# A gated cross-attention and feed-forward layer: the last attention step divided straight into the last two token tiles, and a new list for the end

## The chip, the cores and the metric

The kernel runs on one core of a Trainium2 chip, as one program. The metric is device time in microseconds (us). A core has a matrix engine (PE; its weight loads are shown as PEld), a vector engine (DVE), a scalar engine for activations (ACT), a general engine (POOL) and a queue that issues transfers (SP). Each takes its own instructions strictly in order, and they wait for each other through semaphores. PE writes to PSUM; everything else lies in SBUF or in the chip's main memory.

## The reference

Two gated residual steps over `x` of 32 sequences, 224 tokens, 512 channels, with a context of 750 keys of 384 channels:

```python
x = x + tanh(g_xattn[0]) * xattn(layernorm(x), ctx, mask, Wq, Wkv)   # 16 heads of 32
x = x + tanh(g_ffn[0])   * ffn(layernorm(x), w1, b1, w2, b2)         # 512 -> 2048 -> 512

def bitlinear(x, w, b):
    xq = act_quant(rmsnorm(x))      # 8 bit steps, one scale for each token
    wq = weight_quant(w)            # -1, 0, 1 times one scale
    return einsum('bsd,fd->bsf', xq, wq) + b
def ffn(x, ...): return bitlinear(gelu(bitlinear(x, w1, b1)), w2, b2)
```

Attention of a sequence needs nothing of the others; the feed-forward part works on each token alone.

## The kernel before

**Attention.** A step is one sequence `b` and one group `g` of four heads: 128 steps, numbered 0 to 127. A step has three score rounds. In each, `maxima` computes scores with the queries on the partitions, and DVE takes their row maxima (`mx`); `weights` computes them again with the keys on the partitions, adds the negative maxima (`nT`, turned by `turn_max`), and ACT takes the exponential (`p`), which POOL adds up into `acc`. Both kinds of scores (`sm` and `se` in the profile) use one PSUM tile in turn. `values` multiplies `p` with the values into `po`; `sums` adds `acc` over the partitions with a product with ones, DVE transposes the result to `oT` and takes the reciprocals `rd`; `finish` divides on POOL into `yo`, and `store` writes `yo` with four transfers to the scratch tensor `o_d` in main memory. The main loop (line 1005) interleaves the maxima of step n+1, the weights of step n, the values of step n-1, and the projections of later sequences (`pk`, `pv`, `pq`) in six slots of each step.

**Feed-forward.** The 7168 tokens form 56 tiles of 128, taken in 28 pairs (0 to 27). `ffn_units` gives the work of a pair as named units: `load` of `x` and `o_d` into `xg` and `og`, `add`, `stats`, `rsqrt`, `norm`, `max`, `sa0` to `sa2` (scales), `grid`, `bias`, `round`, `turn` (two transposing transfers), all for both tiles at once; then for each tile t the four column blocks `bt0` to `bt3` of the first product, each evicted by DVE into `h`, `gelut`, `squaret`, `hmt0`, `hmt1` (maxima of the halves), `sbt0` to `sbt2`, `cgridt`, `croundt`, `cturnt`, two halves `ct0` and `ct1` of the second product, and `outt`. The last two pairs borrow tiles of the attention: `x` and `o_d` of pair 27 lie in one tile (`xo` in the profile), and its normalised values and their rounded form in another (`xc`).

**What sets the order.** `Ffn.fill` (line 857) is called in each slot and places units while the slot has room on PE, ACT and DVE. `late` (line 890) widens PE's room by how many tiles are waiting beyond an allowance: 3 everywhere. GELU and exponential need different function tables on ACT, so a `gelu` in the main loop loads one table, computes, and loads the other one back.

After step 126's loop, `drain` (line 895) writes out everything that is left as one list: the weights of step 127 (`top`, `w0` to `w2`), values and sums of steps 126 and 127 (`val`, `vlast`), their divisions and stores (`fin0`, `sto0`, `fin1`, `sto1`), and all units left of pairs 25, 26 and 27. It keeps a clock for each engine, looks up in `TAKES_US` how long each unit takes and on which engine it may run, and takes one unit after the other: among those that can start soonest, the one with the longest chain behind it (`rank`). Where a unit can run on DVE or on POOL or ACT, `small[0]` tells the unit which. `LAST` holds what the units of the attention wait for, `behind` what the units of a pair wait for besides the unit ahead of them. The `fetch` of pair 27's part of `o_d` waits for `sto1`, the last store.

The helper class `Ordered` (line 52 is its call) records every operation, so nearly all instructions in the profile have line 52.

Of the kernel before, what the change touches and what calls it, by code (L numbers as in the profile page):

```python
# [8 lines left out]
F32 = mybir.dt.float32  # L9
# [15 lines left out]
def flamingo_gated_layer(  # L25
# [410 lines left out]
    def finish(b, g):  # L436
# [6 lines left out]
        yo_of[b, g] = yo  # L443

    def store(b, g):
        yo = yo_of.pop((b, g))
        for j in range(HG):
            cols = slice(g * P + j * DH, g * P + (j + 1) * DH)
            sp.dma_start(
                o_d[b * S : (b + 1) * S, cols].rearrange("(c r) d -> r c d", r=DH),  # L450
                yo[j * DH : (j + 1) * DH],
            )
# [67 lines left out]


    draining = []
    NTI = NT // P
    TG = 2
    NF = NTI // TG

    def quant_scales(s, r, amax, n, tag, unit):

        a = smf.tile([P, n], F32, tag=f"{tag}_am", name=f"{tag}_am")
        c = smf.tile([P, n], F32, tag=f"{tag}_c", name=f"{tag}_c")
        s[tag] = c, a
        if n == 1:
            small[0].tensor_scalar(a, amax, r, 1e-5, ALU.mult, ALU.max)
        else:
            small[0].tensor_tensor(a, r, amax, ALU.mult)
            small[0].tensor_scalar(a, a, 1e-5, None, ALU.max)
        yield  # L540
        dve.reciprocal(c, a)
        yield
        if n == 1:
            small[0].tensor_scalar(c, c, 127.0, r, ALU.mult, ALU.mult)
        else:
            small[0].tensor_scalar(c, c, 127.0, None, ALU.mult)
            small[0].tensor_tensor(c, c, r, ALU.mult)
        small[0].tensor_scalar(a, a, unit, None, ALU.mult)
# [7 lines left out]
    def ffn_units(i):  # L556
# [6 lines left out]
        def a_load():  # L563
            if i >= NF - 2:
                both = yp.tile([P, NYC * M], F32, tag="y", name=f"xo_{i}")
                both = both[:, : 2 * TG * D].rearrange("p (a t d) -> p a t d", a=2, t=TG)
                s["xg"], s["og"] = both[:, 0], both[:, 1]
            else:
                s["xg"] = xgp.tile([P, TG, D], F32, tag="xg", name=f"xg_{i}")
                s["og"] = ogp.tile([P, TG, D], F32, tag="og", name=f"og_{i}")  # L570
# [7 lines left out]
        def a_fetch():  # L578
            sp.dma_start(s["og"], o_d[rows, :].rearrange("(t p) d -> p t d", p=P))

# [19 lines left out]
        def a_norm():  # L600
            if i < NF - 2:
                s["xc"] = fp.tile([P, TG, D], F32, tag="xc", name=f"xc_{i}")
            else:
                both = vp.tile([P, NKC * D // 2], F32, tag="v", name=f"xc_{i}")
                s["xc"] = both[:, : TG * D].rearrange("p (t d) -> p t d", t=TG)
                s["xq"] = both[:, TG * D :].bitcast(BF16).rearrange("p (t d) -> p t d", t=TG)
            for t in range(TG):
# [41 lines left out]
        def b_matmul(t, f):  # L649
# [11 lines left out]
            for k in range(NDC):  # L661
# [4 lines left out]
            dve.scalar_tensor_tensor(  # L666
                s["h", t][:, cols], ph, s["qa"][1][:, t : t + 1], b1_sb[:, cols],
                ALU.mult, ALU.add,
# [63 lines left out]
        ]  # L732
        if i == NF - 1:
            first[1:] = [("fetch", 0, "load", 0, 0, 0, a_fetch), ("add", 0, "fetch", 0, 0, 0, a_add)]
        first += [
# [10 lines left out]
            ("turn", 0, "round", 0, 0, 0, a_turn),  # L746
        ]
        parts = [first]
        for t in range(TG):
            part = []  # L750
            for f in range(4):
                part.append((
                    f"b{t}{f}", 0 if f else 3, f"b{t}{f - 1}" if f else "turn", 0.9, 0, 0.75,
                    lambda t=t, f=f: b_matmul(t, f),
# [33 lines left out]
        "sb2": [[("DVE", 0.4)], [("POOL", 0.6)]], "cgrid": [[("DVE", 1.7)], [("POOL", 2.0)]],  # L788
        "cround": [[("ACT", 2.0)], [("DVE", 1.8)]], "cturn": [[("SP", 3.8)]],
        "c": [[("PE", 1.75), ("DVE", 0.5)]], "out": [[("SP", 2.0)]],  # L790
        "top": [[("PE", 0.3), ("ACT", 0.4)]],
        "w": [[("PE", 1.1), ("ACT", 1.7)]],
        "val": [[("PE", 2.9), ("DVE", 0.9)]], "vlast": [[("PE", 4.0), ("DVE", 0.9)]],
        "fin": [[("POOL", 0.6)]], "sto": [[("SP", 3.6)]],
    }

    QUEUE_US = {"sto": 1.9, "turn": 1.9, "cturn": 1.5, "load": 0.5, "fetch": 0.5, "out": 0.4}

# [3 lines left out]
        for name, after in {  # L802
            "w0": "top", "w1": "w0", "w2": "w1", "val": "", "fin0": "val", "sto0": "fin0",
            "vlast": "w2 val", "fin1": "vlast fin0", "sto1": "fin1 sto0",
        }.items()
    }

    class Ffn:
# [3 lines left out]
        def __init__(self):  # L812
            self.slot = 0
            self.parts = []
            self.next = 0
            self.at = {}

        def behind(self, pair, name):
# [3 lines left out]
                "load": [(pair - XG, f"out{TG - 1}"), (pair - 1, "add")],  # L822
                "fetch": [(NF, "sto1")],
                "norm": [(pair - 1, "round")],
# [5 lines left out]
            if name[-1].isdigit():  # L830
                t = int(name[len(name.rstrip("0123456789"))])
                (p1, t1), (ph, th) = (divmod(pair * TG + t - n, TG) for n in (1, HB))
                before = {
                    f"b{t}0": [(pair, "turn")]
                    + [(ph - (pair == NF - 1), f"cround{th}")] * (pair != NF - 2),
# [12 lines left out]
        def ready(self, pair, unit):  # L848
            name, lag, after = unit[:3]
            lag = lag if not draining else 0  # L850
            if after is not None:
# [38 lines left out]
        def late(self, stored, more):  # L890

            ready = stored * S // P - TG * self.next + sum(p[1][-1][0][:3] == "out" for p in self.parts)
            return 0.3 * max(0, ready - (LATE if stored < B - 8 else 3) - more)

        def drain(self, more):
# [3 lines left out]
            draining.append(True)  # L899
            free = {"PE": 0.0, "ACT": 0.0, "DVE": 4.3, "POOL": 5.0, "SP": 0.0}  # L900
            end = {}

            def takes(name):
                kind = name.rstrip("0123456789")
                return TAKES_US.get(kind) or TAKES_US[kind + name[-1]]

            self.parts.insert(0, [NF, more])
            while self.next < NF:
                self.parts += [[self.next, part] for part in ffn_units(self.next)]
                self.next += 1  # L910
            left = {}

            def rank(at):

                if at not in left:
                    left[at] = 0.0
                    left[at] = sum(us for _, us in takes(at[1])[0]) + max(
                        (rank(x) for x in behind if at in behind[x]), default=0.0
                    )
                return left[at]  # L920

            behind = {
                (pair, u[0]): [(pair, u[2] or "")] + self.behind(pair, u[0])
                for pair, units in self.parts for u in units
            }

            def course(at, way):

                t = max(
                    [end.get(x, 0.0) for x in behind[at]  # L930
                     if x[1].rstrip("0123456789") not in ORDER_ONLY or x[1][:-1] != at[1][:-1]],
                    default=0.0,
                )
                t = begin = max(t, free[way[0][0]])
                for engine, us in way:
                    t = max(t, free[engine]) + us
                return begin, t

            while self.parts:
                self.slot += 10  # L940
                found = []
                for part in self.parts:
                    for unit in part[1]:
                        if self.ready(part[0], unit):
                            at = part[0], unit[0]
                            way = min(
                                takes(unit[0]), key=lambda way: course(at, way)[1]
                                + 1.0 * sum(us for engine, us in way if engine == "DVE"),
                            )
                            found.append((course(at, way)[0], -rank(at), part, unit, way))  # L950
                soon = min(f[0] for f in found) + 2
                t, _, part, unit, way = min((f for f in found if f[0] <= soon), key=lambda f: f[1])
                part[1].remove(unit)
                self.at[part[0], unit[0]] = self.slot
                small[0] = {"DVE": dve, "POOL": gp}.get(way[-1][0], act)
                unit[6]()
                for engine, us in way:
                    t = max(t, free[engine])
                    free[engine] = t + (QUEUE_US[unit[0].rstrip("0123456789")] if engine == "SP" else us)
                    t += us  # L960
                end[part[0], unit[0]] = t
                self.parts = [p for p in self.parts if p[1]]
            return end

# [40 lines left out]
    for n in range(N - 1):  # L1005
# [49 lines left out]
        for k in range(6):  # L1055
# [13 lines left out]
            if wunits:  # L1069
                if k in (1, 3, 5):  # L1070
                    wunits.pop(0)()
            else:
                some = ffn.fill(
                    (PE_ROOM[k % 2] - used, (1.1, 2.2)[k % 2], 1.7),
# [18 lines left out]
            for name, at, *do in (  # L1093
                ("val", last[0], values, sums), ("fin0", last[0], finish), ("sto0", last[0], store),
                ("vlast", last[1], values, sums), ("fin1", last[1], finish), ("sto1", last[1], store),
            )
# [40 lines left out]
```

## Time and profile before

| what | value |
| --- | --- |
| time, median of 3 runs | 3007.13 us (3002.2 to 3008.22) |
| the profiled execution | 3006.2 us, span 3004.4 us |
| granted PE clock over the span | 0.991 |
| busy over the span: PE, PEld, DVE, ACT, POOL | 96%, 61%, 57%, 47%, 69% |
| last exponential of step 126 ends | 2905.85 us |
| last sums of step 127 end | 2925.1 us |
| first product of pair 26 begins on PE | 2930.96 us |
| first product of pair 27 begins on PE | 2957.17 us |
| last eviction begins | 3000.96 us |

A timeline line has the start, the busy time, the engine, the operation with what it writes and reads and their shapes, how often it stands there, and in brackets how long the engine was idle before and what ended that. A line of the chain of waits has the start, the length and what the time went to. Names of pair 27's and pair 26's tiles are `xo` and `xc`; `h`, `wq_sb` and `wkv_sb` hold the hidden values of the last three pairs.

### The profile page before, as it was taken

What the parts mean: (1) busy time and instruction counts of PE and PEld (TensorE: products, weight loads), DVE (VectorE), ACT (ScalarE), POOL (GpSimd) and SP (SyncE); (2) the same over time, 40 slices, a digit from 0 to 9 for tenths busy, and PEclk for the clock granted to TensorE, in tenths of its full rate; (3) what the DMA queues carried; (4) which work ended last, traced back from release to release, by engine and by line L of the source; (5) the groups of instructions that cost most, each with busy time, mean ns of one, the idle gap of its engine ahead of it and who ended that gap; (6) DMA issues with size and microseconds to landing.
All of it is one profiled execution on the core that took longest, in us unless ns stands there. A gap on an engine that the chain in (4) does not pass through costs nothing.

```text
span 3004.4 us, 62808 instructions
## 1 busy us (share of the span) xinstructions
PE 2891.3 (96%) x26790; PEld 1839.3 (61%) x26790; DVE 1726.8 (57%) x2583; ACT 1417.8 (47%) x1438; POOL 2087.6 (69%) x2727
## 2 busy tenths in 40 slices
PE   7999999999999999999999999999999999999975
PEld 4665566666666666666666666666666666666643
DVE  5576555655655565555555565655655655555545
ACT  2344454544545455445445454544544554545444
POOL 3465867767766777777667777767767777687674
PEclk9999999999999999999999999999999999999997
DMA  4333222223222223221222222123221132321213
GB/s 147 89 112 99 53 57 47 57 67 62 55 66 46 56 59 74 68 60 32 63 69 50 65 56 63 45 64 73 50 60 46 45 74 63 74 72 23 45 45 79
DMA packets 352696, 190.02 MB, mean 63 GB/s; under 512 B 282144, under 2 KB 305056, under 8 KB 352288
## 3 DMA queue, kind: packets, MB, share of 16 engines
q1 hardware_dynamic: 352416, 186.01, 25.6%
q8 instruction: 209, 3.42, 0.5%
q14 instruction: 71, 0.58, 0.1%
HBM read 119.86 MB, written 29.39 MB: 50 GB/s over the span
## 4 chain that ended last, share of the span: by engine, by line
PE 82%; ACT 10%; POOL 3%; DVE 3%; DMA 1%; issue 1%; SPq 0%; POOLq 0%; ACTq 0%; DVEq 0%
PE po L52 17%; PE pk L52 14%; PE se L52 14%; PE sm L52 12%; PE pv_None L52 7%; ACT p L52 7%; PE ph L52 6%; PE pv L52 6%; PE pq L52 3%; DVE mx L52 2%; ACT L52 2%; POOL acc L52 1%; ACT h L52 1%; PE pn L52 1%; POOL h L52 0%
## 5 line engine op out<-in xcount | busy, mean ns | idle before, releaser
L52 POOL TENSOR_TENSOR acc<-acc,p 125x896 f32<-125x896 f32 x510 | 1068.4, 2095 | 322.5 <-ACT p L52 301.2
L52 DVE TENSOR_REDUCE mx<-sm 112x4 f32<-112x2000 f32 (+1 forms) x384 | 861.1, 2243 | 662.6 <-PE sm L52 662.6
L52 ACT ACTIVATE p<-se 125x1792 f32<-125x1792 f32 x384 | 639.1, 1664 | 758.1 <-PE se L52 708.6
L52 PE MATMUL pk<-y,wkv_sb 128*128 128x375 f32 x1536 | 541.8, 488 | 9.7 <-DMA y<-in_ctxT 9.7
L52 PE MATMUL sm<-kT,qT 32*112 32x500 f32 (+1 forms) x4096 | 427.3, 509 | 33.9 <-ACT p L52 23.3
L52 POOL TENSOR_TENSOR acc<-p 125x896 f32<-125x896 f32 x128 | 268.1, 2095 | 247.9 <-ACT p L52 247.8
L52 PEld LDWEIGHTS pk<-y,wkv_sb 128*128 128x128 f32 x1536 | 279.5, 190 | 182.7 <-issue 44.4
L52 PE MATMUL se<-qT,kT 32*125 32x224 f32 x6144 | 360.3, 349 | 0.0
L52 PE MATMUL po<-p,v 125*32 125x224 f32 x6144 | 318.1, 355 | 0.0
L52 PE MATMUL pv<-wkv_sb,y 128*125 128x256 f32 x1248 | 312.5, 387 | 0.0
L52 PEld LDWEIGHTS se<-qT,kT 32*125 32x125 f32 x6144 | 296.0, 183 | 0.0
L52 PEld LDWEIGHTS sm<-kT,qT 32*112 32x112 f32 x4096 | 159.4, 170 | 193.4 <-ACT p L52 138.7
L52 PEld LDWEIGHTS po<-p,v 125*32 125x32 f32 x6144 | 186.9, 110 | 119.5 <-issue 44.0
L52 PEld LDWEIGHTS pv<-wkv_sb,y 128*125 128x125 f32 x1248 | 223.9, 188 | 53.1 <-issue 18.3
L52 ACT COPY kT<-pk 128x375 f32<-128x375 f32 x256 | 120.2, 470 | 277.4 <-PE pk L52 276.6
L52 PE MATMUL pv_None<-wkv_sb,y 128*125 128x256 f32 x1056 | 250.9, 387 | 0.0
L52 PEld LDWEIGHTS pv_None<-wkv_sb,y 128*125 128x125 f32 x1056 | 191.2, 187 | 89.4 <-issue 60.2
L52 PE MATMUL po<-w2q,hT 128*128 128x256 fp8e4 x1792 | 220.2, 278 | 25.8 <-DMA hT<-hq 25.8
L52 DVE SCALAR_TENSOR_TENSOR h<-ph,qa_am,b_sb 128x512 f32<-128x512 f32 x216 | 158.9, 745 | 138.6 <-PE ph L52 110.6
L52 PE MATMUL ph<-w1q,xT 128*128 128x512 fp8e4 x896 | 226.0, 384 | 4.8 <-DMA xT<-xc 4.8
L52 PE MATMUL pq<-xTb,wq_sb 128*128 128x224 f32 x1024 | 221.8, 359 | 1.1 <-DVE wq_sb L52 0.7
L52 PEld LDWEIGHTS <-hT 128*128 128x128 bf16 x1792 | 171.1, 100 | 76.8 <-issue 27.8
(129 smaller groups left out, 2860.3 us busy)
## 6 DMA issues: line engine op xcount, KB each, us to landing
y<-in_ctxT SPq DMA_DIRECT2D x31, 1125.0 KB, 6.7
x<-in_x SPq DMA_DIRECT2D x32, 448.0 KB, 7.3
xTb<-in_xT SPq DMA_DIRECT2D x32, 448.0 KB, 3.7
o_d<-yo SPq DMA_DIRECT2D x512, 28.0 KB, 1.6
xg<-in_x SPq DMA_DIRECT2D x26, 512.0 KB, 3.7
og<-o_d SPq DMA_DIRECT2D x26, 512.0 KB, 4.6
out<-xg SPq DMA_DIRECT2D x52, 256.0 KB, 2.6
wa<-in_w1T SPq DMA_DIRECT2D x8, 512.0 KB, 7.2
```

The source lines that it names most:

```text
L52: return lambda *args, **kw: tc.keep_in_program_order(build(*args, **kw))
```

## The change

- `finish_last(t)` takes the place of `finish` and `store` for step 127. It divides `oT` by `rd` in blocks of 32 tokens by 32 channels straight into the place in the last pair's `og` where they belong: tile 0 with 12 operations on DVE (`fin1`), tile 1 with 16 on ACT (`fin2`). `sto1` is gone.
- `a_fetch` of pair 27 gets the first three head groups of both tiles in one transfer, and the last group of 32 older rows in a second one; it waits for `sto0` alone.
- The first units of pair 27 are split by tile: `add` for the three fetched groups, then for each tile `ladd`, `lstats`, `lrsqrt`, `lnorm`, `lmax`, `lsa0` to `lsa2`, `lgrid`, `lround`, `lturn`.
- `drain` no longer takes one unit after the other for good: `course` makes a whole list for a ranking, and out of 1700 rankings, the first 200 drawn at random around `rank` and the others altered from the best one so far, the list with the earliest modelled end is kept. The model of `course` also slows PE after an idle time.
- `late` allows 1.5 instead of 3 for the last eight sequences. `closing` keeps `gelu` units out of the last two slots of step 126.

The built lists differ as follows. Before begins its end with `top`, `w0`, `val`, `load` of pair 27, `w1`, `w2`, and has `b12`, `b13`, `square0` and all after them of pair 25 left. After begins with `load` of pair 27, `val`, `norm` of pair 26, `top`, `w0`, `w1`, and has `cround0` and the scales of tile 1 of pair 25 left. SP's order after is: load of pair 27, four stores of step 126, transpose of tile 0 of pair 25, fetch of pair 27 (two transfers), transposes of pair 26.

```diff
+    def finish_last(t):
+        b, g = steps[-1]
+        oT, rd = po_of[b, g]
+        first = b * S - (NF - 1) * TG * P
+        for c in range(S // DH):
+            at = first + c * DH
+            if at // P != t:
+                continue
+            for j in range(HG):
+                rows = slice(j * DH, (j + 1) * DH)
+                cols = slice(g * P + j * DH, g * P + (j + 1) * DH)
+                to = last_o[0][at % P : at % P + DH, t, cols]
+                if t == 0:
+                    dve.tensor_scalar(to, oT[rows, 0, c, :], rd[rows, c : c + 1], None, ALU.mult)
+                else:
+                    act.activation(to, oT[rows, 0, c, :], AF.Identity, scale=rd[rows, c : c + 1])
...
         def a_fetch():
-            sp.dma_start(s["og"], o_d[rows, :].rearrange("(t p) d -> p t d", p=P))
+            of = o_d[rows, :].rearrange("(t p) d -> p t d", p=P)
+            if i < NF - 1:
+                sp.dma_start(s["og"], of)
+                return
+            sp.dma_start(s["og"][:, :, : D - P], of[:, :, : D - P])
+            old = (B - 1) * S - i * TG * P
+            sp.dma_start(s["og"][:old, 0, D - P :], of[:old, 0, D - P :])
+        def l_add0():
+            cols = slice(0, D - P)
+            small[0].tensor_tensor(
+                s["xg"][:, :, cols], s["xg"][:, :, cols], s["og"][:, :, cols], ALU.add
+            )
+        def l_add(t):
+            cols = slice(D - P, D)
+            small[0].tensor_tensor(
+                s["xg"][:, t, cols], s["xg"][:, t, cols], s["og"][:, t, cols], ALU.add
+            )
+        def l_rsqrt(t):
+            ve = smf.tile([P, 1], F32, tag="ve2", name=f"ve2_{i}_{t}")
+            s["nm", t] = smf.tile([P, 1], F32, tag="nm2", name=f"nm2_{i}_{t}")
+            small[0].tensor_scalar(s["nm", t], s["mv", t][:, 0:1], -1.0, None, ALU.mult)
+            small[0].tensor_scalar(
+                ve, s["mv", t][:, 1:2], 1.0 + EPS, EPS * EPS, ALU.mult, ALU.add
+            )
+            s["r", t] = rsqrt(smf, ve, 1, P, "r2")
+        def l_turn(t):
+            if "xT" not in s:
+                kT = kp.tile([P, M], F32, tag="kT", name=f"xT_{i}")[:, : TG * D // 2]
+                s["xT"] = kT.bitcast(BF16).rearrange("p (t c n) -> p t c n", t=TG, c=NDC)
+            sp.dma_start_transpose(s["xT"][:, t], s["xq"][:, t, :])
...
     LAST = {
-            "vlast": "w2 val", "fin1": "vlast fin0", "sto1": "fin1 sto0",
+            "vlast": "w2 val", "fin1": "vlast fin0", "fin2": "vlast fin0",
...
-                "fetch": [(NF, "sto1")],
+                "fetch": [(NF, "sto0")],
...
+                    f"ladd{t}": [(NF, f"fin{1 + t}")],
...
         def ready(self, pair, unit):
             name, lag, after = unit[:3]
+            if name[:4] == "gelu" and self.closing:
+                return False
...
-            return 0.3 * max(0, ready - (LATE if stored < B - 8 else 3) - more)
+            return 0.3 * max(0, ready - (LATE if stored < B - 8 else 1.5) - more)
...
+            rng = random.Random(1)
+            every, best = sorted(todo), None
+            for n in range(1700):
+                if n < 200:
+                    like = {at: rank(at) + rng.uniform(0.0, 12.0) * (n > 2) for at in every}
+                    args = (0.4, 1.0, 2.0)[n % 3], rng.choice((0.3, 0.6, 1.0))
+                else:
+                    like, args = dict(best[2]), best[3]
+                    for at in rng.sample(every, rng.choice((1, 2, 4, 8))):
+                        like[at] += rng.uniform(-15.0, 15.0)
+                us, order = course(like, *args)
+                if best is None or us <= best[0]:
+                    best = us, order, like, args
...
+                ffn.closing = n == N - 2 and k > 3
...
-                ("vlast", last[1], values, sums), ("fin1", last[1], finish), ("sto1", last[1], store),
+                ("vlast", last[1], values, sums), ("fin1", (0,), finish_last),
+                ("fin2", (1,), finish_last),
```

## The prediction

> **What bounds the kernel now.** I read the table of busy time by stretches first.
>
> ```profile
> 2723.00:2811.00 88.00, 87.84 (x827) 56.11 (x820) 47.67 (x69) 39.45 (x39) 60.89 (x74) 1.00 0.22 46
> 2811.00:2901.00 90.00, 80.94 (x794) 50.32 (x793) 50.82 (x78) 45.86 (x46) 68.55 (x93) 0.94 0.17 38
> 2901.00:3004.40 103.40, 62.07 (x489) 37.93 (x487) 50.45 (x92) 49.41 (x37) 54.76 (x107) 0.83 0.28 64
> ```
>
> The columns are the stretch, its length, and the busy time of PE, PEld, DVE, ACT and POOL, then the clock granted to PE. Until 2811 us PE is busy 87.8 of every 88 us: work added there lengthens the run by its own length, and only work that leaves PE shortens it. In the last 103 us no engine is busy more than 62: there latencies decide. So the change acts on two bills, PE's time before the end and the chain of waits in it.
>
> Then the timeline around the hand-over to the end, the last exponential of step 126:
>
> ```profile
> 2904.19 1.66 ACT L52 ACTIVATE p<-se 125x1792 f32<-125x1792 f32 x1 [3.59 <-PE se L52]
> 2905.87 1.28 ACT L52 ACT_TABLE_LOAD   x1
> 2906.00 4.23 POOL L52 TENSOR_TENSOR acc<-acc,p 125x896 f32<-125x896 f32 x2 [2.23 <-ACT p L52]
> 2907.17 1.91 ACT L52 ACTIVATE h<-h 128x2048 f32<-128x2048 f32 x1
> 2909.09 1.28 ACT L52 ACT_TABLE_LOAD   x1
> 2910.50 0.33 ACT L52 COPY nT<-pn 128x224 bf16<-128x224 bf16 x1
> 2910.88 0.41 PE L52 MATMUL se<-nT,ones 3*125 3x448 bf16 x4 [4.88 <-ACT nT L52]
> ```
>
> A GELU between exponentials brings two table loads; the copy of the turned maxima stands behind it, and PE waits 4.88 us. From the end of the exponential to the next `se` it is 5.03 us. After that wait PE is slow.
>
> ```profile
> 2912.64 3.44 PE L52 MATMUL po<-p,v 125*32 125x224 f32 x48
> 2928.48 2.50 SPq L52 DMA_TRANSPOSE xT<-xc  x2
> 2930.96 8.91 PE L52 MATMUL ph<-w1q,xT 128*128 128x512 fp8e4 x31 [4.83 <-DMA xT<-xc]
> 2934.30 0.38 SPq L52 DMA_DIRECT2D xo<-o_d  x1
> 2938.24 2.37 POOL L52 TENSOR_TENSOR xo<-xo 128x1024 f32<-128x1024 f32 x1 [7.99 <-DMA xo<-o_d]
> ```
>
> The same 48 matmuls of `values` take 2.48 us elsewhere. Pair 26 starts at 2930.96, 2.47 after its first transpose was issued; pair 27 gets its attention output at 2938.24, 3.94 after its issue; the span ends at 3004.4, that is 73.4 after pair 26 starts. Last, the chain of waits:
>
> ```profile
> 2988.31 0.27 POOL qb_c L52
> ...
> 2990.93 2.01 ACT hq L52
> 2992.96 4.25 DMA hT<-hq
> 2997.26 3.68 PE po L52 x32
> 3000.96 0.48 DVE xo L52
> ```
>
> Scales, grid, rounding, transpose, last product: this tail returns in the changed kernel unchanged.
>
> **The change, part by part.** I lay the changed kernel's order, with what each instruction waits for, along these rows. All times are on the clock of the span of before.
>
> *Less held back.* By the end of step 124 the changed order has issued two half products of pair 24 (1.92 each) and two column blocks of pair 25 (0.93 each) that before had not: 5.7 us of PE. PE is full there; in steps 123 and 124 I grant 0.3 of idle. So +5.4. Step 125 then carries six such blocks (5.7) where before had none, but before stood idle in it 1.85, 2.37 and 1.84 us in three waits and ran its last `se` at the low clock (1.81 for what takes 0.98). The blocks fit there: 0. Step 126 starts at 2882.55 + 5.4 = 2887.95.
>
> *Nothing left for step 126.* Before fills it with 9.5 us of PE work and takes 23.3. Now no filler is left, and its own chain shows. The GELU of tile 0 sits at the end of step 125, so the stall of 5.03 is moved, not removed; first exponential done 5.0 + 3.6 (2910.88 to 2914.48) = 8.6 in. Then maxima at the low clock 2.0 (row at 2882.55, after a gap of 1.84), values and sums 3.8 (2912.64 to 2916.46), `se` 1.2, exponential 1.67 with two handovers of 0.1: the second exponential ends at 17.4, 2905.35. At full clock it would be 15.4.
>
> *`val` ahead of `top`.* The list now starts with the values and sums of step 126. The sums wait for POOL's `acc`; PE runs in order, so turn, weights and all of step 127 queue behind. On POOL: two adds for the second exponential 4.3, the inverse root of pair 26 in 14 small operations 4.4 (2890.63 to 2894.97), two adds for the third 4.3: 2918.4. In before, `top` and a score group went ahead of that wait. Then sums at the low clock 0.85, turn and copy 0.8, score group and exponential 3.6, the next `se` 2.17 and exponential 1.8: second exponential of step 127 done at 2927.7. Before: 2919.35. At full clock 1 less.
>
> *The output of step 126 and the fetch.* `fin0` stands on POOL behind both adds of that exponential (4.35) and takes 0.6: 2932.65. Behind it on SP: four stores at 0.444, the transpose of pair 25 (1.8), the fetch of three heads' groups (3.94 as at 2934.30; bounds 3.7 and, if the transpose ahead holds it, 6.3). The fetch of the old 32 rows waits for the landing of the first, since both are taken as writes to one tile; so it is issued at 2940.2, and behind it on SP waits the turn of pair 26. The small fetch lands in some 2.0 (bounds 1.6, a 28 KB store, and 4.3, the slower of the two loads of a gate), hidden behind the turn. PE begins with tile 1 of pair 26, the second transpose: 0.4 + 1.26 + 2.47 gives 2944.3. That is 13.3 later than before.
>
> *Direct division.* Removed: `fin1` on POOL, four stores 1.99, the wait for them 1.23. Added: 12 divisions of 32x32 on DVE, 16 on ACT. No row has them; pitch between 0.10 (independent scale operations at 2944.86 to 2945.11 come 0.13 apart) and 0.33 (the copy of 128x224 on ACT); I take 0.17 by the former: 2.0 on DVE, bounds 1.2 and 4. ACT's 16 (up to 5.3) lie under the wait for pair 26, since ACT has nothing else then; uncovered they would cost up to 5.3. DVE's wait for POOL's add of the fetched part (1.8, done 2944.0) and, by the list, for the first block of pair 26.
>
> *Tile by tile.* From 2944.3: first block at the low clock and its eviction 2.75 (2930.96 to 2933.70), divisions 2.0, four evictions 3.3, statistics of tile 0 0.9: 2953.3. Two inverse roots of one column follow each other on POOL, 3.55 each (ten operations, as at 2957.58), where before has one of 4.4, and the grid of tile 0 stands behind both: 7.1. Grid 0.7, rounding 0.65, one transpose 2.5: tile 0 is at PE at 2964.25. Before: 2957.15 for both. Four blocks at the low clock to the last eviction 6.45: 2970.7. From there DVE is dense: four evictions 3.3, four half maxima 4.9, two product evictions 1.0, one inverse root 2.4, small ones 1.0: 12.6, to 2983.3. Product eviction, scales and grid of tile 0 3.6; inverse root of tile 1 on POOL 3.6; its scales and grid 2.9; rounding 2.05; transpose 4.3; products 3.7; last eviction to the end of the span 3.44: 3006.9.
>
> **Sum.** Up to PE's pair 26 +13.3; from there 62.6 instead of 73.4, -10.8. Together +2.5 on 3004.4. The profiled execution took 3006.2 and the median is 0.9 above it: 3007.13 + 2.5, about 3009. What a measurement of this kernel tells from no change is 0.2%, 6 us: 3001.1 to 3013.1 is no change.
>
> The rows say that a wait of 1.84 keeps the clock low (2882.55). The Trainium skill, "TensorE: Matmul & The Clock Gate", Part 1, states that the array falls to half clock after an idle window of about 3.4 us and is back after one busy window. By that rule alone the short waits inside steps 126 and 127 would not cost anything, and the sum would be about 3 us lower, an estimate.
>
> **The rivals.** *Faster.* PE stays at full clock (-2.0 in step 126, -1.0 in 127, -1.8 in each of the two groups of four blocks: 8.9 for 31 products against 7.1 at 0.23 each, the 1.83 for 8 at 2897.58), the divisions come at 0.10 (-0.8), and a third of DVE's dense stretch falls into waits (-4). -11.4: 2998. For it: DVE is busy under half the time in the end. Against it: after each wait above 2.4 us the trace shows the low clock.
>
> *Slower.* Transposes and copies in SP's queue hold each other. For it: the stores issued behind a transpose at 2878.70 took 2.71 instead of 1.77. Price: fetch +2.4, small fetch +2.3 with the turn behind it, and in the tail, where transposes of three tiles follow each other, some 1.3: +6.0, 3015. It decides from +3.6 on. Against it: plain fetches in the end landed in 3.94.
>
> *The hold-back costs nothing*, because PE has hidden slack: -5.4, 3004, still no change. 87.84 of 88 speaks against it.
>
> **How the numbers follow.** Forecast 0.38 (own range 3003 to 3013), costless hold-back 0.07, faster 0.26, slower 0.29. Faster by over 0.2%: 0.26; within: 0.45; slower: 0.29. The range reaches into both: 2996 to 3018.
>
> **What would show it.** In the profile after: PE busy but for a few tenths up to step 125; the first exponential of step 127 near 2922; the big fetch issued near 2936 and the small one only after it landed; pair 26 starting near 2944; DVE dense from 2970. Wrong it is if the fetch is issued before 2930, if the sums of step 126 don't wait for POOL, or if from pair 26 to the end it takes less than 58 or over 68 us.

## The result, and the profile after

| | kernel before | changed kernel |
| --- | --- | --- |
| median | 3009.07 us (15 runs, 3002.20 to 3011.47) | 3012.6 us (15 runs, 3010.12 to 3021.76) |
| ratio to before | | 1.0019, 95% interval 1.0012 to 1.0025 |
| profiled execution | 3006.2 us, span 3004.4 | 3010.12 us, span 3008.3 |
| step 125 / step 126 starts | 2861.59 / 2882.55 | 2870.34 / 2890.87 |
| pair 26 begins on PE | 2930.96 | 2947.38 |
| from there to the end of the span | 73.4 | 60.9 |

By the ratio the change costs 0.19%, 5.7 us. That is inside the 0.2% that the prediction called no change, but the interval leaves out 1: the loss is small, but there. The profiled execution of the changed kernel is the fastest of its 15, which matters below. The ratios leave out one execution, of 15224 us, of the kernel with the division ahead and the old rows first.

The table of busy time by stretches of the changed kernel; the columns are the stretch, its length, busy PE, PEld, DVE, ACT and POOL, the granted clock, the share of the DMA engines and GB/s:

```profile
2723.00:2811.00 88.00, 86.14 (x781) 54.57 (x783) 52.21 (x82) 46.43 (x48) 63.98 (x75) 1.00 0.24 46
2811.00:2901.00 90.00, 82.60 (x804) 51.99 (x796) 49.42 (x70) 42.99 (x42) 61.68 (x67) 0.97 0.16 38
2901.00:3008.30 107.30, 65.23 (x558) 40.83 (x550) 55.02 (x115) 50.51 (x53) 62.46 (x124) 0.80 0.27 60
```

In the first stretch PE was busy 87.84 of 88 us before; now it has 1.86 us of idle time where it should have almost none. The last stretch looks as before: no engine is full.

The timeline of the changed kernel around the start of step 126 (start, busy time, engine, operation, and in brackets the idle time ahead and what ended it):

```profile
2889.15 1.66 ACT L53 ACTIVATE p<-se 125x1792 f32<-125x1792 f32 x1 [4.83 <-PE se L53]
2892.13 1.91 ACT L53 ACTIVATE h<-h 128x2048 f32<-128x2048 f32 x1
2895.46 0.33 ACT L53 COPY nT<-pn 128x224 bf16<-128x224 bf16 x1
2895.84 0.41 PE L53 MATMUL se<-nT,ones 3*125 3x448 bf16 x4 [3.66 <-ACT nT L53]
2899.45 2.02 PE L53 MATMUL sm<-kT,qT 32*112 32x250 f32 x16 [1.86 <-ACT p L53]
```

The GELU of tile 0 now stands behind step 125's last exponential, which ends at 2890.81; the next `se` starts 5.03 us later, the very stall that stood a step later before. Then the hand-over to the end:

```profile
2916.69 4.23 POOL L53 TENSOR_TENSOR acc<-acc,p 125x896 f32<-125x896 f32 x2
2920.97 0.98 PE L53 MATMUL po<-acc,ones 125*32 125x224 f32 x8 [3.39 <-POOL acc L53]
2930.60 4.25 POOL L53 TENSOR_TENSOR acc<-acc,p 125x896 f32<-125x896 f32 x2 [1.90 <-ACT p L53]
2934.82 0.55 POOL L53 TENSOR_TENSOR yo<-oT,rd 128x224 f32<-128x224 f32 x1
2939.42 4.08 SPq L53 DMA_DIRECT2D xo<-o_d  x2
2943.61 2.50 SPq L53 DMA_TRANSPOSE xT<-xc  x2
2950.09 2.96 DVE L53 TENSOR_SCALAR xo<-oT,rd 32x32 f32<-32x32 f32 x12
```

The sums of step 126 wait for POOL; its division `yo` stands behind POOL's adds of an exponential of step 127; both fetches take the queue from 2939.42 to 2943.50, since the second is held until the first has landed; only then is pair 26 turned. The 12 direct divisions take 0.246 us each.

Two things come late because the list has them there. The rounded values of pair 26 were ready long before its turn was issued, and DVE was idle ahead of the first block of pair 26, behind which the divisions stand:

```profile
2929.88 0.69 DVE L53 TENSOR_SCALAR xc<-xc 128x1024 bf16<-128x1024 f32 x1
2944.85 1.80 POOL L53 TENSOR_TENSOR xo<-xo 128x768 f32<-128x768 f32 x1 [3.34 <-issue]
2949.30 0.75 DVE L53 SCALAR_TENSOR_TENSOR wkv_sb<-ph,qa_am,b_sb 128x512 f32<-128x512 f32 x1 [11.50 <-PE ph L53]
```

The rounding ends at 2930.57, 13 us before the turn; POOL's add, which the divisions wait for too, ends at 2946.65, 3.4 us before them. No run below puts the turn ahead of the fetch, or the divisions ahead of that first block. Last, the end of the chain of waits, the same tail as before:

```profile
2994.78 2.01 ACT hq L53
2996.80 4.24 DMA hT<-hq
3001.09 3.68 PE po L53 x32
3004.80 0.48 DVE xo L53
```

### The profile page after: what moved, and what is told of

It is laid out like the page before. It is cut to its first block, busy times and chain, and to the rows that moved or that the text cites. A ratio compares the mean times of both kernels' runs of the same rounds, so it can differ in the third digit from the quotient of the medians.

```text
span 3008.3 us, 62864 instructions
## 1 busy us (share of the span) xinstructions
PE 2893.3 (96%) x26790; PEld 1840.2 (61%) x26790; DVE 1732.7 (58%) x2610; ACT 1422.0 (47%) x1453; POOL 2089.8 (69%) x2726
## 4 chain that ended last, share of the span: by engine, by line
PE 80%; ACT 10%; POOL 3%; DVE 3%; DMA 2%; issue 1%; SPq 0%; POOLq 0%; ACTq 0%; DVEq 0%
PE po L53 16%; PE pk L53 14%; PE se L53 14%; PE sm L53 12%; PE pv_None L53 7%; ACT p L53 7%; PE ph L53 6%; PE pv L53 6%; PE pq L53 3%; DVE mx L53 2%; ACT L53 1%; POOL acc L53 1%; ACT h L53 1%; POOL h L53 1%; PE pn L53 1%
```

## The experiments

Times are compared through each kernel's ratio to the kernel before on the same chip; 0.0001 is 0.3 us. Positions are counted from the start of step 126 where a run's early part differs by a microsecond or two.

**The changed kernel again**, as a measure for its neighbours.

> The changed kernel itself, as the measure for the runs beside it: 1.0019 of the kernel before (3010 to 3015), step 125 starting 8 to 9 us later than in the kernel before, pair 26 some 56.5 us after the start of step 126, the span ending 60.9 us after that.

Measured: 3016.17 us, 1.0019 (1.0011 to 1.0028). Step 125 starts at 2871.42, pair 26 57.6 us after the start of step 126, and the span ends 64.8 us after that, not 60.9. The ratio repeats; the tail does not. Two executions of one program differ by 3.9 us in it. The timeline of the first, then of the second:

```profile
2982.97 3.67 PE L53 MATMUL po<-w2q,hT 128*128 128x256 fp8e4 x32 [2.99 <-DMA hT<-hq]
3001.09 3.67 PE L53 MATMUL po<-w2q,hT 128*128 128x256 fp8e4 x32 [1.08 <-DMA hT<-hq]
```

```profile
2985.95 5.08 PE L53 MATMUL po<-w2q,hT 128*128 128x256 fp8e4 x32 [2.98 <-DMA hT<-hq]
3005.48 5.33 PE L53 MATMUL po<-w2q,hT 128*128 128x256 fp8e4 x32 [2.46 <-DMA hT<-hq]
```

The same 32 products after the same wait, 2.99 and 2.98, take 3.67 or 5.08 us: the granted clock there is 1.00 in the one and 0.71 in the other.

**The hold-back alone.** The kernel before with one number changed:

```diff
-            return 0.3 * max(0, ready - (LATE if stored < B - 8 else 3) - more)
+            return 0.3 * max(0, ready - (LATE if stored < B - 8 else 1.5) - more)
```

> The kernel before with the allowance of late at 1.5 alone; its main loop then places every unit where the changed kernel does, and its end is the old kind of list on shorter leftovers. Theory (the hold-back is not free and was sized too small): step 125 starts near 2870.3 as in the changed kernel, 8.7 later than before, step 126 gives 6 of it back by having no filler, and the old list does the rest: 3006 to 3012, within 0.2% of before. Rival (the hold-back costs nothing, the new end loses the time): step 125 starts late but the end has less work, and the run is 4 to 8 us faster than before, 2999 to 3004. Rival (the price is carried to the end): 8 us slower than before, 3015 to 3018.

Measured: 3015.4 us, 1.0022 (1.0013 to 1.0030), 6.6 us slower than before, as the second rival had it. The start of step 125 is late as expected; that the end gives it back is refuted. From the start of step 126 to the end of the span it takes 121.4 us, before 121.85, though PE has 64 products fewer to do there (596 against 660).

Where the time goes is read from windows over the same stretch of work: from the start of step 97, the first in which the two orders differ, to the start of step 125. The kernel before, then this one:

```profile
2226.41:2861.59 635.18, 628.98 (x5881) 401.91 (x5880) 369.48 (x555) 321.05 (x328) 461.26 (x616) 1.00 0.24 56
```

```profile
2226.68:2872.05 645.37, 635.62 (x5922) 405.65 (x5921) 373.45 (x565) 323.73 (x328) 468.50 (x628) 1.00 0.25 58
```

10.19 us longer: 6.64 of it is work of PE that was moved ahead, 3.55 is new idle time (9.75 against 6.20). The changed kernel has the same window, 645.38 long with 635.62 busy, in both of its profiles, so `closing`, which this run lacks, alters nothing up to there. The idle time lies in steps for which too few blocks are left. One such stretch of the changed kernel, a table line and the two waits in it:

```profile
2724.13:2745.55 21.42, 19.93 (x191) 12.87 (x190) 13.13 (x19) 13.84 (x16) 15.43 (x16) 1.00 0.17 31
```

```profile
2727.60 0.41 PE L53 MATMUL se<-nT,ones 3*125 3x448 bf16 x4 [0.87 <-DVE mx L53]
2735.52 0.41 PE L53 MATMUL se<-nT,ones 3*125 3x448 bf16 x4 [0.41 <-ACT nT L53]
```

In the kernel before, the same stretch of 21.99 us has no idle time, and 11 products more (202 against 191).

**The hold-back undone.** The changed kernel with 3 in place of 1.5; the list is picked anew.

> The changed kernel with the allowance back at 3; its main loop is before's, the list of the end is picked anew on before's leftovers. Theory (hold-back priced too low): step 125 starts near 2861.6 as before; 3004 to 3008, some 4 to 6 us faster than the changed kernel. Rival (the new end loses the time, whatever the hold-back): within 2 us of the changed kernel, 3010 to 3014.

Measured: 3006.48 us, 0.9995 (0.9986 to 1.0004), 7.2 us less than the changed kernel by the ratios. Step 125 starts at 2862.53. With the run above each of the two parts has been tried with and without the other: the hold-back costs 6.6 us with the old end and 7.2 with the new one; the new end gains 1.5 us with the old allowance and 0.9 with the new one, both within the intervals.

**More allowance.** The other direction, 4.5, with two edits that are told further down (division ahead, old rows first).

```diff
-            return 0.3 * max(0, ready - (LATE if stored < B - 8 else 1.5) - more)
+            return 0.3 * max(0, ready - (LATE if stored < B - 8 else 4.5) - more)
```

> The changed kernel with the allowance at 4.5 instead of 1.5, the early division and the early old rows; the list is picked anew. By the end of step 124 it has issued 13.3 us less of blocks and half products than with the allowance at 3, and leaves all of pair 25 and a part of 24 to the end. Theory A (each unit of allowance is worth some 4.6 us, as between 1.5 and 3): 2996 to 3001. Theory B (the end fills up: what is left out of a full PE comes back on DVE, ACT and POOL in the end, which are busy about half of it): the start of step 125 is 11 to 14 us earlier than in the kernel before, and the end grows by as much or more: 3005 to 3015.

Measured: 3020.75 us, 1.0042 (1.0028 to 1.0056). Step 125 starts at 2852.21, 9.4 us earlier than before, and the end grows by far more: 144.7 us from the start of step 126.

```profile
2873.90:3018.60 144.70, 89.21 (x696) 53.60 (x696) 77.37 (x146) 72.08 (x68) 87.27 (x178) 0.79 0.32 72
```

Theory A is refuted. Theory B has the direction, but neither of its sizes: step 125 starts less early than its 11 to 14 us, and the time lies above its 3005 to 3015. No engine is full there either; the end has more chains to run, since pair 25 now begins its blocks in it as well. With the two edits in each, the allowances 1.5, 3 and 4.5 give 1.0000, 0.9988 and 1.0042: 3 is the best of them, ahead of 1.5 by no more than the intervals.

**Values behind the first scores.** The changed kernel's own list, one unit moved:

```diff
             us, order = best[:2]
+            at_of = {at: way for at, way in order}
+            def behind_of(what, of):
+                order.remove((what, at_of[what]))
+                order.insert(order.index((of, at_of[of])) + 1, (what, at_of[what]))
+            behind_of((NF, "val"), (NF, "w0"))
```

> The changed kernel's own list with one unit moved: values and sums of step 126 stand behind the first weights of step 127 instead of ahead of turn and weights. Theory (the wait of the sums for POOL blocks all of step 127 on PE): the first se of step 127 starts near 2912 instead of 2922.7, the division of step 126 near 2925 instead of 2934.8, pair 26 starts near 2938 instead of 2947.4; 3002 to 3006, 6 to 10 us faster than the changed kernel. As my prediction priced this wait, only 2.9 us of it are to be had, 3009 to 3010. Rival (the end is bound by the work of DVE and POOL behind it): pair 26 starts earlier but the span ends within 2 us of the changed kernel.

Measured: 3009.94 us, 1.0005 (0.9996 to 1.0013). By the ratios that is 4.2 us below the changed kernel, but its end is only 0.6 us shorter in the profiles, 116.8 against 117.4, so how much of it the move is worth is not settled. What is settled is that the theory's order of events did not come about:

```profile
2919.07 1.32 ACT L53 ACTIVATE xc<-xo,nm 128x512 f32<-128x512 f32 x2
2920.29 0.33 ACT L53 COPY nT<-pn 128x224 bf16<-128x224 bf16 x1
2920.68 0.64 PE L53 MATMUL se<-nT,ones 3*125 3x448 bf16 x4 [4.88 <-ACT nT L53]
2934.69 0.56 POOL L53 TENSOR_TENSOR yo<-oT,rd 128x224 f32<-128x224 f32 x1
```

The wait for POOL is gone, and PE waits 4.88 us for the copy `nT` instead: the list has a square and a normalisation ahead of it on ACT. The first `se` comes at 2920.68, not 2912, and the division stays where it was, because on POOL it still stands behind the adds; pair 26 starts 56.0 us after step 126 instead of 56.5.

**Old rows first.** The small fetch (`old_rows[0]`) is issued right behind the load of pair 27, and the unit `fetch` keeps the big one:

```diff
                 todo[at][6]()
+                if at == (NF - 1, "load"):
+                    old_rows[0]()
```

> The changed kernel's own list; the small fetch of 32 old rows is issued right behind the load of pair 27, far ahead of the big one. Theory (the small fetch waits for the landing of the big one, and the turn of pair 26 stands behind it on the queue): the turn is issued near 2939.9 instead of 2943.6, pair 26 starts near 2943.8 instead of 2947.4; 3008 to 3010, 2.5 to 3.7 us faster than the changed kernel. Rival (the transfers share the engines, the turn lands no earlier): pair 26 starts within 1 us of 2947.4 and the time is unchanged.

Measured: 3013.42 us, 1.0010 (1.0001 to 1.0018). In the timeline the queue is free again after one fetch:

```profile
2940.72 0.99 SPq L53 DMA_DIRECT2D xo<-o_d  x1
2941.82 2.51 SPq L53 DMA_TRANSPOSE xT<-xc  x2
```

Counted from step 126, the turn is issued at 49.97 instead of 52.74, pair 26 starts at 54.07 instead of 56.51, and the span ends at 114.8 instead of 117.4. The theory's mechanism holds in the profile, with 2.4 to 2.8 us where it had 2.5 to 3.7; the ratios say 2.7, with intervals that overlap.

**The division ahead.** Again one unit of the changed kernel's own list is moved:

```diff
+            behind_of((NF, "fin0"), (NF, "w0"))
```

> The changed kernel's own list with one unit moved: the division of step 126 on POOL stands behind the first weights of step 127, ahead of the add for the second, instead of behind it. Theory (the fetch, and the turn of pair 26 behind it on the queue, hang on this division, which waits on POOL for an exponential it does not need): the division runs near 33 us after the start of step 126 instead of 44, the turn is issued near 41 instead of 52.7, pair 26 starts on PE as soon as the sums of step 127 are through, near 46.5 instead of 56.5; the whole end moves with it: 3001 to 3005, 8 to 10.5 us faster than the changed kernel. Rival (DVE and POOL behind it are full and set the end): pair 26 starts as early, but the time gains under 4 us.

Measured: 3010.2 us, 1.0004 (0.9995 to 1.0013), 4.5 us below the changed kernel.

```profile
2928.01 2.08 POOL L53 TENSOR_TENSOR acc<-p 125x896 f32<-125x896 f32 x1 [2.98 <-ACT p L53]
2930.05 0.56 POOL L53 TENSOR_TENSOR yo<-oT,rd 128x224 f32<-128x224 f32 x1
2935.97 3.60 SPq L53 DMA_DIRECT2D xo<-o_d  x2
2939.68 2.50 SPq L53 DMA_TRANSPOSE xT<-xc  x2
```

The division runs at 37.8, not 33: it still stands behind the add of `w0`'s own exponential. The turn is issued at 47.4 instead of 52.7 and pair 26 starts at 51.2 instead of 56.5. The division is on the path, for 5.3 us up to pair 26, half of what the theory had. From there the end took 64.9 us, as in the second execution of the changed kernel, so that from step 126 to the end of the span this profile is only 1.3 us shorter (116.1 against 117.4). Whether DVE and POOL hold back the rest, as the rival says, or the clock does, is not settled.

**Division ahead and old rows first**, both edits on the changed kernel's list.

> Both edits on the changed kernel's own list: the division of step 126 ahead of the second add, and the small fetch of old rows issued behind the load of pair 27. Theory (with the division ahead, the turn comes before PE is through with step 127, and the wait between the two fetches is hidden): within 1 us of the kernel with the division ahead alone, 3000 to 3004. Rival (the two waits add up): 2.5 us faster than that kernel, 2998 to 3002.

Measured: 1.0000 (0.9991 to 1.0009), median 3010.46. The turn is issued at 44.1, pair 26 starts at 48.1, 3.1 earlier than with the division alone, and the span ends at 110.4 in the profile. The two waits add up there, as the rival had it, because the division did not come early enough to hide the second one. Both expected times were missed by 8 us and more, and the ratios, 1.2 us apart, can't confirm the gain.

**Divisions made twice.** Each of the 12 on DVE is issued two times:

```diff
                 if t == 0:
+                    dve.tensor_scalar(to, oT[rows, 0, c, :], rd[rows, c : c + 1], None, ALU.mult)
                     dve.tensor_scalar(to, oT[rows, 0, c, :], rd[rows, c : c + 1], None, ALU.mult)
```

> The changed kernel with each of the 12 divisions of tile 0 on DVE made twice; the output is the same. Theory (they stand on the path between the first block of pair 26 and the statistics of tile 0): 24 at a pitch of 0.246 take 5.9 us instead of 3.0, the statistics begin 2.9 us later behind pair 26's start, and the time grows by 2.5 to 3 us, 1.0027 to 1.0030 of the kernel before. Rival (DVE has slack there): the time grows by less than 1 us, 1.0019 to 1.0022.

Measured: 3020.24 us, 1.0032 (1.0021 to 1.0043).

```profile
2953.18 6.19 DVE L53 TENSOR_SCALAR xo<-oT,rd 32x32 f32<-32x32 f32 x24
```

24 take 6.19 us instead of 2.96, and the turn of tile 0 comes 20.9 us after pair 26 starts instead of 17.7: the 3.2 us are all on the path, in the place that the list gives them. The ratio, 3.9 us up, agrees but is too wide to measure it.

**The first list.** The changed kernel without the search:

```diff
-            for n in range(1700):
+            for n in range(1):
```

> The changed kernel with the first ranking's list, without the search of 1700; all else as changed. By the planner's own model its end is 23.65 us longer than the picked list's (96.65 against 73.0): 3032 to 3038. My theory (the model leaves out POOL's adds of the exponentials, and this list has the division of step 126 ahead of the second weights): what the search gains on the chip is a fraction of that, 3010 to 3020. Rival (the search picks worse lists than the first): faster than the changed kernel by over 3 us, 3004 to 3009.

Measured: 3037.21 us, 1.0094 (1.0080 to 1.0108): 22.6 us slower than the changed kernel, where the planner's model says 23.65. My theory and its rival both fall. This list has the division early (38.5) and still takes 139.5 us from the start of step 126, against 117.4 and 122.5. So with the first list the parts that were split by tile are far worse than the old end, and this one difference the planner's model had right.

**The old allowance, division ahead, old rows first.**

```diff
-            "w0": "top", "w1": "w0", "w2": "w1", "val": "", "fin0": "val", "sto0": "fin0",
+            "w0": "top", "w1": "w0 fin0", "w2": "w1", "val": "", "fin0": "val", "sto0": "fin0",
```

> The changed kernel with the allowance back at 3, the division of step 126 bound ahead of the second weights in the list, and the old rows fetched early; the list is picked anew. Theory (the two bills add: 8.6 us for the hold-back, and the early division): step 125 starts near 2862, 2997 to 3003, the best so far. Rival (with the allowance at 3 the leftovers of pair 25, its last blocks, two gelus and half maxima, set the end instead, as where the list was picked anew with the allowance at 3 the span ran 75.8 us behind pair 26's start): no gain over that kernel, 3004 to 3008.

Measured: 3006.32 us, 0.9988 (0.9979 to 0.9997): faster than both kernels, but by 3.6 us on before, 9.3 below the changed kernel where 7.2 for the hold-back and 5.7 for the two edits would be 12.9. The bills don't add, and the median lies in the range of the rival: against the kernel with the allowance undone alone the ratios give 2.1 us, within the intervals. In its profile the end takes 121.7 us.

**The adds in the model, and a longer search.** On top of that:

```diff
+                    if at[1] in ("w0", "w1"):
+                        free["POOL"] = max(free["POOL"], t) + (2.1, 4.25)[at[1] == "w1"]
...
-            for n in range(1700):
+            for n in range(10000):
```

> The kernel with the allowance at 3, the early division and the early old rows, and two edits in the planner: its model of POOL also counts the adds of the first two exponentials of step 127 (2.1 and 4.25 us), and it alters 10000 orders instead of 1700. Theory (the planner's model holds on the chip, as the 22.6 us between the first and the picked list showed, and what it leaves out is POOL's adds): some 2 us faster than the same kernel without these two edits, 3002 to 3006, 0.998 to 0.9985 of the kernel before. Rival (at this size of difference the model says nothing): within 0.9980 to 1.0005 of the kernel before, no better than without.

Measured: 2995.85 us, 0.9956 (0.9943 to 0.9970), 13.2 us faster than before and 18.9 below the changed kernel. It gains far more than expected. Its timeline:

```profile
2912.54 2.07 POOL L53 TENSOR_TENSOR acc<-p 125x896 f32<-125x896 f32 x1
2914.58 0.56 POOL L53 TENSOR_TENSOR yo<-oT,rd 128x224 f32<-128x224 f32 x1
2918.33 0.38 SPq L53 DMA_DIRECT2D xo<-o_d  x1
2921.02 2.50 SPq L53 DMA_TRANSPOSE xT<-xc  x2
```

```profile
2884.84:2994.30 109.46, 73.72 (x660) 45.41 (x660) 68.14 (x139) 56.87 (x56) 67.30 (x116) 0.87 0.29 64
```

The division comes at 29.7 from step 126, the turn at 36.2, and pair 26 starts at 40.6, with no wait but 0.17 us: the turn is through when PE comes to it. Without the two edits the division came at 34.9 and pair 26 at 48.4. The end takes 109.5 us at a mean clock of 0.87, where the changed kernel has 0.80 and 0.76 in its two profiles. Which of the two edits brings it, the adds in the model or the longer search, was not tried apart.

## Why the prediction was right, and by which steps

The time (3012.6 against 3009, within 2996 to 3018) and the verdict came out. That alone says little: the range is wide, and most kernels of this document lie in it. Against the profiled spans the sum said +2.5 and the trace has +3.9; by the ratio it is +5.7. Step by step, in positions from the start of step 126 on:

| step of the prediction | predicted | measured |
| --- | --- | --- |
| step 126 starts later than before by | 5.4 | 8.3; from step 97 on 9.8 |
| second exponential of step 126 ends | 17.4 | 17.1 |
| sums of step 126, held by POOL | 30.5 | 30.1 |
| division of step 126 done | 44.7 | 44.5 |
| big fetch issued | 48.3 | 48.6 |
| pair 26 begins on PE | 56.4 | 56.5 |
| pair 26 to the first product of pair 27 | 20.0 | 20.2, again 20.1 |
| pair 26 to the end of the span | 62.6 | 60.9, again 64.8 |

The order of waits from step 126 to pair 26 was right, and in the first profile each position between them to half a microsecond (in the second pair 26 begins at 57.6): the GELU's stall moved a step ahead and kept its 5.03, the sums waited for POOL (3.39), the fetch left at 2939.42, the small one after it, the turn behind both. What pair 26 loses, its tail gives back in part: by 8.6 to 12.5 us, where I had 10.8. Six profiles with the new end and the allowance of 1.5 have tails of 60.7 to 64.9 us, the two with the old end 73.4 and 73.0. Of the signs that I named, one failed, PE busy but for a few tenths up to step 125; the times on the clock came some 3 us later for the same reason.

**The term that was mis-sized is the hold-back.** "PE is full there; in steps 123 and 124 I grant 0.3 of idle. So +5.4." It measured 10.2 us at the start of step 125, counted from step 97; on the clock of the profiles it is 8.75, because this execution came to step 97 1.45 us earlier. I counted which blocks were issued by the end of step 124 and took it that a full PE passes that on unchanged. The count was right, 40 products more, but PE is busy 6.64 us longer with the moved work where I had 5.7, and the rest is idle time. The smaller allowance draws the waiting tiles down from step 97 on, later steps find fewer blocks to put into PE's waits, and 3.55 us of new idle time appear, all of it before step 123: from step 100 on a step has up to 1.2 us, where the kernel before has up to 0.4. I looked for the slack in the two steps ahead of the end only.

That step 125 would take in its six blocks at no cost came out: it is 20.5 us long, before 21.0. With 9.8 instead of 5.4 in its first term the sum would have been 4.4 us higher.

**The hold-back is the whole loss.** Alone it costs 6.6 us and undone it returns 7.2. The direct division and the tile by tile end, which most of my working went into, are worth 0.9 to 1.5 us together with their list, less than its intervals can tell from nothing. So the rival "the hold-back costs nothing" is refuted twice, and the slower rival by its place: the fetch was issued at 48.6 where I had 48.3, pair 26 followed as forecast, and the loss was PE's.

**The divisions.** Predicted 2.0 us on DVE, 0.17 for each by rows of small scale operations, bounds 1.2 and 4; measured 2.96, all on the path. ACT's 16 took 5.27 (up to 5.3 forecast) and were hidden under the wait for pair 26.

**`val` ahead of `top`.** The wait was there, 3.39 us, but taking it away moved pair 26 by 0.5 us only: PE then waited 4.88 us for ACT's copy, and the division still stood behind POOL's adds.

**The clock.** The faster rival was argued down with "after each wait above 2.4 us the trace shows the low clock". The changed kernel's trace does not bear that out: after a wait of 2.99 the products ran at 1.00.

**The anchor and two slips.** 2 of the 3.6 us between forecast and median come from the anchor: 3007.13 was the median of three runs of the kernel before, over 15 it is 3009.07. By its own terms the sum is 3009.6, not 3009. The 8 products that the faster rival takes at 1.83 stand in their row, at 2897.51, with 1.90; that moves its 2998 by half a microsecond.

## What to carry to other kernels

Work taken ahead into a full engine can cost more than its own length: here it used up the stock that fills the small waits of all steps until then, so compare the idle time over the whole stretch, from the first step that differs. The end need not give that time back where it is held by waits and not by the engine that was relieved. A unit that waits in another engine's queue for something it doesn't need (here a division behind the adds of a later exponential) is found by asking, for each link of the hand-over, what stood ahead of it; moving one such unit gains until the next one holds. The 13 us came with the allowance back at 3, the division and the old rows early, POOL's adds in the model and a longer search, all together. That the planner put the division behind POOL's adds because its model leaves them out is likely, but not shown: the adds and the longer search came in together.

## What the runs showed of the hardware

- The clock granted to PE in a stretch of short bursts is not fixed by the program: 32 products took 3.67 or 5.08 us after equal waits in two executions, and the tails of the two differ by 3.9 us, at a granted clock of 0.89 and 0.83. Of the 26 times of the changed kernel 13 lie at 3010 to 3014 us and 13 at 3016 to 3022. The Trainium skill, "TensorE: Matmul & The Clock Gate", Part 1, says that the window in which activity is measured runs freely, so that the same kernel has differing stretches at the low clock; these runs show such differences, though not that the window is their cause.
- Score products took 2.02 us after a wait of 1.86 in the changed kernel (2899.45), where they take 1.11 at full clock; ahead of that lay a wait of 3.66 us and 1.8 us of work. In the kernel before, `se` took 1.81 us instead of 0.93 at 2878.90, after waits of 1.85 and 2.37 us with 1.1 us of work between them, and the scores behind a further wait of 1.84 still took 2.02. So PE is found at the low clock behind short waits too, as the prediction had it by the rows; that such waits cost nothing, as the page's figure in the prediction alone would have it, these rows don't show.
- A division of 32 by 32 takes 0.246 us on DVE and 0.33 on ACT, though a scale and round of 128 by 512 on DVE takes no more than 0.44 (two in 0.87 at 2928.97): with a sixteenth of the elements in each partition the small piece still takes over half the time. The Trainium skill, "VectorE: DVE Perf Modes", in its section on the errata, puts it down to a fixed cost for each instruction; the rows agree.
